# Two graph layers of 32 batches on one core: a norm's scaled mean computed on GpSimd in place of VectorE

## The chip, the core and the metric

The kernel runs on one core of a Trainium2 chip. A core has five engines, each with an instruction queue of its own that is worked off in order: TensorE (PE in the profile) for matmuls and transposes, VectorE (DVE) and ScalarE (ACT) for elementwise work and reductions, GpSimd (POOL) for small elementwise work and for issuing indirect DMAs, and SyncE (SP) for issuing plain DMAs. Engines wait for each other through semaphores. The metric is the time of one execution on the device in microseconds (us); the time of a kernel is the median of its runs.

## What is computed

The input x has 32 batches of 512 rows of 512 numbers, all float32; a matrix adj of 512 x 512 zeros and ones (on average 4 ones per row) says which rows see which. Two layers follow each other, each with a residual:

```python
h = jnp.maximum(_layernorm(x, axis=-1), 0.0)
x = x + _L0_gnn_ref(h, adj, Wq, bq, Wk, bk, Wv, bv, Wo, bo)   # 8-head attention over neighbours, out @ Wo + bo
h = jnp.maximum(_layernorm(x, axis=-1), 0.0)
x = x + _L1_gnn_ref(h, W, a, beta, adj)                       # softmax of leaky_relu(s1_i + s2_j) * adj; elu(h' + beta * h)
```

The layer norm has no weights: `(x - m) / sqrt(v + 1e-5)`, with the mean and the variance of a row. So each row needs two numbers, rstd = (v + 1e-5)^-0.5 and -m * rstd; then relu(x * rstd + (-m * rstd)) is one ScalarE instruction with a scale and a bias per row. There are 32 batches x 4 tiles x 2 layers = 256 such norms of 128 rows.

## The kernel before

Rows are sorted once by their number of neighbours, so that the neighbours of a tile of 128 rows fit into 4 gathers of 128 rows. Everything is then done for tiles of 128 rows, 4 tiles (T) a batch, 32 batches (B).

Stage A of a batch (line 767 on, `turned_state`, `queries`, `keys_and_values`): a tile of x is fetched by an indirect DMA from POOL (line 774), normed (`norm`), passed through relu on ACT (line 768) and transposed on PE (line 741, copied to SBUF by ACT at line 796). Queries are one product with Wq (line 42, bias added by DVE at line 804). Keys and values of two tiles are made together by a Strassen scheme of seven half products (line 872), with sums of the left sides on DVE (line 861) and additions of results on DVE (line 880) and copies on ACT (lines 894, 896). All three go to tables in DRAM (SP, line 911).

Stage B of a batch: for each tile, POOL gathers key and value rows (line 960, tile `kv`) and query rows (line 983, tile `qe`) edge by edge. DVE multiplies and sums (lines 1028, 1031), ACT takes the exponential (1037) and weighs the values (1042), PE sums the edges (line 1015 into bank `px`), DVE divides (1070, 1066), PE transposes (741) and multiplies with Wo (42), DVE adds the residual (1083). Then comes the second norm, relu into `hx` (768), two dot products on DVE (1091), and a store to a table (1097). Layer 1 runs two batches behind: its edge weights (lines 1157 to 1170, tile `wv`), its edge sums (1015), transposes, product with W (42), the elu (1232 on ACT, 1237 and 1238 on DVE) and an indirect store of the result from POOL (779). In the last batches the rows' s1 values go through DRAM and come back spread over partitions (lines 1130 to 1143).

The order of all this is not written by hand. The program describes each operation with `op(engine, cost, key, function, r=, w=)`: the engine, an assumed duration, a due time, and the buffers that it reads and writes. `Plan.order` then runs a list scheduler over all operations: it keeps an assumed clock for each engine, takes whichever operation can start first, prefers low keys among those that can start at the same time, and assigns the buffers of each ring as they come free. What it returns is the issue order of every engine. Inside one operation several instructions can follow each other on one engine; nothing comes between them. A change of an operation's cost, engine or number moves the assumed clocks, and so can move instructions all over the program.

The norm is three operations. The first, on DVE, is `stats`: lines 756 (statistics of 512 columns into `st`), 757 (mean and variance into columns 0 and 1 of `mv`) and 758 (variance plus epsilon into column 2). The second, on POOL, raises column 2 to the power -0.5 (line 761; `mhalf` holds -0.5). The third, on DVE again, writes column 3 = column 0 * -1 * column 2 (line 763). ACT's relu (line 768) takes column 2 as scale and column 3 as bias. The last reader of `mv` in a batch is line 1121 on DVE, which checks that mean and variance of all four tiles are finite. `mv` has 4 columns for each tile of a batch; a planned wait is for the tile's columns.

Of the kernel before, what the change touches and what calls it, by code (L numbers as in the profile page):

```python
# [12 lines left out]
ALU = mybir.AluOpType  # L13
# [51 lines left out]
class Plan:  # L65
# [14 lines left out]
    def buf(self, tag, name=""):  # L80
        return Buf(tag, name)

    def op(self, eng, us, key, fn, r=(), w=(), dma=0, form=128):
        def parts(xs):
            return [x if isinstance(x, tuple) else (x, None) for x in xs]

        r, w = parts(r), parts(w)
        o = Op(eng, us * self.PACE.get(eng, 1.0), key, fn, r, w, [], dma)
        o.form = form
        evict = eng in ("DVE", "ACT") and any(b.tag in self.free_order for b, _ in r + w)  # L90
        o.rank = key - self.FREE * evict
        for xs, write in ((r, False), (w, True)):
            for b, part in xs:
                for other, opart, owrite in b.log:
                    if (write or owrite) and other is not o and (
                        part is None or opart is None or part == opart
                    ):
                        o.before[other] = True
                b.log.append((o, part, write))
        for b in dict.fromkeys(b for b, _ in r + w):  # L100
            b.users += 1
            if b.first is None and b.tag in self.rings:
                b.first = o
                o.alloc.append(b)
            elif b.first is not None and b.first is not o:
                o.behind[b.first] = True
        self.ops.append(o)
        return o
# [110 lines left out]
def kernel(  # L219
# [23 lines left out]
    nc = tc.nc  # L243
# [7 lines left out]
    def ctile(shape, name, dt=F32):  # L251
        return const.tile(shape, dt, name=name, tag=name)

    wq, wk, wv, wo, w1 = (ctile([P, C, D], n) for n in ("wq", "wk", "wv", "wo", "w1"))
    mhalf = ctile([P, T], "mhalf")
# [50 lines left out]
    buf, op = plan.buf, plan.op  # L306
# [444 lines left out]
    def norm(key, src, mv, t, name):  # L751

        s6 = buf("st", name)

        def stats():
            nc.vector.bn_stats(s6.ap, src.ap)  # L756
            nc.vector.bn_aggr(mv.ap[:, t, 0:2], s6.ap)
            nc.vector.tensor_scalar_add(mv.ap[:, t, 2:3], mv.ap[:, t, 1:2], EPS)  # L758

        op("DVE", 1.05, key, stats, r=[src], w=[s6, (mv, t)])  # L760
        op("POOL", 0.75, key, lambda: nc.gpsimd.tensor_tensor(  # L761
            mv.ap[:, t, 2:3], mv.ap[:, t, 2:3], mhalf[:, 0:1], op=ALU.pow), w=[(mv, t)])
        op("DVE", 0.17, key, lambda: nc.vector.scalar_tensor_tensor(  # L763
            mv.ap[:, t, 3:4], mv.ap[:, t, 0:1], -1.0, mv.ap[:, t, 2:3], op0=ALU.mult, op1=ALU.mult),
           w=[(mv, t)])

    def relu(dst, src, mv, t):
        nc.scalar.activation(dst, src, AF.Relu, bias=mv[:, t, 3:4], scale=mv[:, t, 2:3])  # L768
# [13 lines left out]
    def turned_state(b, t, key, mv):  # L782
        xb = buf("x", f"x{b}_{t}")
        if b:
            op("POOL", 1.3, key - 2.0 * S, lambda: fetch(xb.ap, b, t), r=[C_["perm"]], w=[xb], dma=P * D * 4)
        else:
            op("SP", 0.1, -90.0 + 0.01 * t, lambda: nc.sync.dma_start(xb.ap, x[0, ts(t, P), :]), w=[xb], dma=P * D * 4)
        norm(key - 1.3 * S, xb, mv, t, f"a{b}_{t}")
        op("ACT", 0.8, key - 0.9 * S, lambda: relu(xb.ap, xb.ap, mv.ap, t), r=[(mv, t)], w=[xb])
        pt, hT = buf("D", "pt"), buf("hT", f"hT{b}_{t}")  # L790
        kt = key + ((0.48, -0.51)[t % 2] if b else -0.51) * S
        if b == 0 and t == 0:
            run_on(kt, 3, pt, first, 1.7)
        o = op("PE", 0.45, kt, lambda: turned(pt.ap, xb.ap), r=[xb], w=[pt])
        plan.reserve(o, hT)
        op("ACT", 0.6, kt, lambda: nc.scalar.copy(hT.ap.rearrange("p c q -> p (c q)"), pt.ap), r=[pt], w=[hT])  # L796
        return hT
# [222 lines left out]
    def layer0(b, t, kb, slots, held, qs, weights):  # L1020
# [61 lines left out]
        op("PE", 3.43, k + 0.72 * S, lambda: dense(pw.ap, oT.ap, wo), r=[oT, C_["wo"]], w=[pw])  # L1082
        op("DVE", 0.7, k + 0.9 * S, lambda: nc.vector.tensor_tensor(x1.ap, pw.ap, x1.ap, op=ALU.add), r=[pw], w=[x1])  # L1083
        norm(k + 0.9 * S, x1, s["mv1"], t, f"b{b}_{t}")
        hx = s["hx"][t] = buf("hx", f"hx{b}_{t}")
        op("ACT", 0.8, k + 1.0 * S, lambda: relu(hx.ap[:, 1 : D + 1], x1.ap, s["mv1"].ap, t),
# [404 lines left out]
```

## Time and profile before

| | |
|---|---|
| median of 3 runs | 2706.05 us (2705.66 to 2709.75) |
| profiled execution | 2724.4 us |
| its span, first to last instruction | 2722.6 us |
| granted PE clock, mean | 0.989 |
| busy PE / DVE / ACT / POOL | 98% / 75% / 71% / 67% |
| DMA | 790 MB, 290 GB/s over the span |

The profile is that of one execution. Busy time of PE counts modelled ends of pipelined matmuls, so the busy time of weight loads (PEld) is given too. "Idle before" an instruction is the time that its engine stood still before it, with what ended that idleness after the arrow. "issue" is time in which the engine waited for nothing that the profile shows. In a timeline, a row is the start in us, the duration, the engine, the line, the operation with its output and inputs, how many are merged into the row, and in brackets the idle time before it. In a table of stretches, a row is the stretch in us, its length, and then the busy time of each engine with the number of instructions, the mean granted clock of PE (1.00 is full), the share of the DMA engines' time, and GB/s. Two instructions of one engine can overlap by some tens of nanoseconds in a timeline.

### The profile page before, as it was taken

Reading aid. Unit: us, or ns where it says so; the run is one execution under the profiler, and the core shown is the slowest. Engines: PE = TensorE matmul, PEld = TensorE weight load, DVE = VectorE, ACT = ScalarE, POOL = GpSimd, SP = SyncE. Lnnn points to the kernel's source line nnn. Section 1 sums busy time; section 2 is a strip of 40 time slices with the busy share of each in tenths; the row PEclk is TensorE's granted clock in tenths of the full one; section 3 lists DMA queues with packets and bytes.
Section 4 is the critical chain, followed back from the end, with each engine's and each line's share of the span. In section 5 each row is a group of like instructions: output and inputs, shape, how many; then the busy total and the mean of one; then the engine's idle time right before and its main releaser. Section 6 shows DMA issues by size and latency. Waiting matters only on the chain.

```text
span 2722.6 us, 39798 instructions
## 1 busy us (share of the span) xinstructions
PE 2657.9 (98%) x10248; PEld 1216.0 (45%) x10248; DVE 2054.8 (75%) x5209; ACT 1931.4 (71%) x6183; POOL 1818.6 (67%) x1710
## 2 busy tenths in 40 slices
PE   9999999999999999999999999999999999999986
PEld 4444444444444444444444444444444444444432
DVE  7767777777777777777777777777777777777674
ACT  1557777687776777777777777777777777777772
POOL 2776766667766766666766766766666766666673
PEclk9999999999999999999999999999999999999998
DMA  5988888889888888888888888988888988988883
GB/s 180 259 282 315 295 301 304 285 297 311 300 296 300 298 295 315 290 293 312 300 303 303 302 296 299 312 298 295 313 296 288 323 291 299 315 292 284 304 259 107
DMA packets 237457, 790.08 MB, mean 290 GB/s; under 512 B 34667, under 2 KB 34675, under 8 KB 237222
## 3 DMA queue, kind: packets, MB, share of 16 engines
q0 software_dynamic: 156736, 644.99, 70.4%
q1 hardware_dynamic: 80486, 142.48, 14.0%
q8 instruction: 83, 1.36, 0.2%
q14 instruction: 152, 1.25, 0.1%
HBM read 617.88 MB, written 169.46 MB: 289 GB/s over the span
## 4 chain that ended last, share of the span: by engine, by line
PE 88%; issue 3%; POOL 3%; DVE 2%; DMA 2%; ACT 1%; another core or an unknown queue 0%; POOLq 0%; SPq 0%; DVEq 0%; ACTq 0%
PE pd L42 46%; PE pd L872 26%; PE pd L741 6%; PE pd L1015 4%; PE px L1015 4%; POOL kv L960 1%; PE pd L932 1%; PE pd L1111 1%; DMA qe<-qtab,qidx 1%; POOL qe L983 1%; DMA x<-in_x_dram,perm 1%; POOL x L774 0%; ACT kv L1042 0%; DMA kv<-tkv,idx 0%
## 5 line engine op out<-in xcount | busy, mean ns | idle before, releaser
L1042 ACT ACTIVATE kv<-kv 128x64 f32<-128x64 f32 x4096 | 1012.0, 336 | 5.2
L983 POOL DMA_INDIRECT qe<-qtab,qidx x512 | 546.8, 1068 | 229.9 <-issue 123.2
L960 POOL DMA_INDIRECT kv<-tab,idx x480 | 513.0, 1069 | 180.6 <-issue 119.6
L42 PE MATMUL pd<-wq,hT 128*128 128x512 f32 x1024 | 466.4, 599 | 1.3 <-ACT hT L796 1.3
L42 PE MATMUL pd<-wo,oT 128*128 128x512 f32 x1032 | 464.5, 593 | 0.0
L42 PE MATMUL pd<-w,gT 128*128 128x512 f32 x992 | 446.4, 593 | 1.4 <-DVE gT L1221 1.4
L774 POOL DMA_INDIRECT x<-in_x_dram,perm x252 | 352.0, 1397 | 85.8 <-issue 46.4
L1028 DVE TENSOR_TENSOR qe<-qe,kv 128x1024 f32<-128x1024 f32 x256 | 312.6, 1222 | 41.2 <-DMA qe<-qtab,qidx 23.4
L1031 DVE TENSOR_REDUCE s<-qe 128x16 f32<-128x1024 f32 x256 | 310.9, 1216 | 0.1
L42 PEld LDWEIGHTS pd<-wq,hT 128*128 128x128 f32 x1024 | 196.1, 193 | 246.0 <-issue 243.2
L42 PEld LDWEIGHTS pd<-wo,oT 128*128 128x128 f32 x1032 | 194.8, 190 | 240.0 <-issue 222.4
L42 PEld LDWEIGHTS pd<-w,gT 128*128 128x128 f32 x992 | 188.1, 190 | 239.7 <-issue 231.2
L761 POOL TENSOR_TENSOR mv<-mv,mhalf 128x1 f32<-128x1 f32 x256 | 171.1, 669 | 174.7 <-DVE mv L758 150.7
L779 POOL DMA_INDIRECT out_dram<-w,perm x128 | 158.5, 1238 | 153.2 <-DVE w L1238 120.1
L872 PE MATMUL pd<-wk,hT 128*128 128x512 f32 x496 | 241.5, 611 | 4.0 <-ACT hT L796 3.4
L872 PE MATMUL pd<-wt,S 128*128 128x512 f32 x496 | 237.7, 602 | 3.8 <-DVE k L880 3.7
L872 PE MATMUL pd<-wv,S 128*128 128x512 f32 x496 | 235.2, 597 | 4.1 <-DVE mv L763 2.1
L1232 ACT ACTIVATE w<-pd,dn 128x512 f32<-128x512 f32 x128 | 87.7, 685 | 178.0 <-PE pd L42 163.6
L1091 DVE CUSTOM_DVE_ANT_0 w<-hx,wa_r 128x512 f32<-128x512 f32 x256 | 175.5, 686 | 9.3 <-ACT hx L768 8.6
L756 DVE BATCH_NORM_STATS2 st<-x 128x6 f32<-128x512 f32 x256 | 176.5, 689 | 3.0 <-DMA x<-in_x_dram 0.4
L1083 DVE TENSOR_TENSOR x<-pd,x 128x512 f32<-128x512 f32 x128 | 88.1, 688 | 119.8 <-PE pd L42 86.5
L741 PEld LDWEIGHTS pd<-ident,w 128*128 128x128 f32 x1152 | 133.5, 142 | 82.7 <-issue 46.8
(213 smaller groups left out, 3569.6 us busy)
## 6 DMA issues: line engine op xcount, KB each, us to landing
qtab<-q SPq DMA_DIRECT2D x124, 258.0 KB
tab<-hx SPq DMA_DIRECT2D x120, 260.0 KB
tab<-v SPq DMA_DIRECT2D x120, 260.0 KB
tab<-k SPq DMA_DIRECT2D x120, 256.0 KB
qe<-qtab,qidx POOLq DMA_INDIRECT x512
kv<-tab,idx POOLq DMA_INDIRECT x480
x<-in_x_dram,perm POOLq DMA_INDIRECT x252
th<-hx SPq DMA_DIRECT2D x8, 260.0 KB
```

Source lines behind the costliest of these rows:

```text
L42: nc.tensor.matmul(out, lhsT, rhs, start=start, stop=stop)
L741: nc.tensor.transpose(p[:, ts(c, P)], src[:, ts(c, P)], ident)
L756: nc.vector.bn_stats(s6.ap, src.ap)
L774: nc.gpsimd.indirect_dma_start(dst, None, rows, bass.IndirectOffsetOnAxis(ap=perm[:, t : t + 1], axis=0), **lim)
L872: nc.tensor.matmul(p.ap, lhs()[:, c, :], rhs[:, c, :], start=first and c == 0, stop=c == K2 - 1, skip_group_check=True)
L960: nc.gpsimd.indirect_dma_start(dst, None, tab.ap, bass.IndirectOffsetOnAxis(ap=idx[:, t, g : g + 1], axis=0), bounds_check=N + DUMMY - 1, ...
L983: op("POOL", 1.3, kb - 0.84 * S + 0.1 * g, lambda q=qs[g // 2], g=g, t=t: nc.gpsimd.indirect_dma_start(q.ap[:, g % 2, :], None, s["qtab"]. ...
L1015: nc.tensor.matmul(out(g), lhs(g), row(slots, g, c0, n), start=True, stop=True)
L1028: nc.vector.tensor_tensor(qe.ap[:, :, 0:D], qe.ap[:, :, 0:D], sl.ap[:, :, KO : KO + D], op=ALU.mult)
L1031: nc.vector.tensor_reduce(sb.ap, qe.ap[:, :, 0:D].rearrange("p n (h f) -> p n h f", f=HD), axis=AX.X, op=ALU.add)
L1042: nc.scalar.activation(p[:, h, 0:HD], p[:, h, 0:HD], AF.Copy, scale=p[:, h, HD : HD + 1])
L1091: nc.vector.tensor_tensor_reduce(scr.ap, hx.ap[:, 1 : D + 1], row, 1.0, 0.0, op0=ALU.mult, op1=ALU.add, accum_out=dst)
```

## The change

The third operation is gone. DVE now writes column 3 = column 0 * -1 * 1 as a fourth instruction of `stats`, before the power exists, and POOL multiplies column 3 by column 2 right behind its power, in the same operation. So column 3 is complete when POOL is done, and ACT waits for POOL alone. The planner's costs change with it: `stats` from 1.05 to 1.2, POOL's operation from 0.75 to 1.3, and DVE's 0.17 is dropped. The file is two lines longer: lines behind the norm are numbered two higher after the change; the power is line 763 and the product line 764.

```diff
             nc.vector.bn_aggr(mv.ap[:, t, 0:2], s6.ap)
             nc.vector.tensor_scalar_add(mv.ap[:, t, 2:3], mv.ap[:, t, 1:2], EPS)
 
-        op("DVE", 1.05, key, stats, r=[src], w=[s6, (mv, t)])
-        op("POOL", 0.75, key, lambda: nc.gpsimd.tensor_tensor(
-            mv.ap[:, t, 2:3], mv.ap[:, t, 2:3], mhalf[:, 0:1], op=ALU.pow), w=[(mv, t)])
-        op("DVE", 0.17, key, lambda: nc.vector.scalar_tensor_tensor(
-            mv.ap[:, t, 3:4], mv.ap[:, t, 0:1], -1.0, mv.ap[:, t, 2:3], op0=ALU.mult, op1=ALU.mult),
-           w=[(mv, t)])
+            nc.vector.tensor_scalar(mv.ap[:, t, 3:4], mv.ap[:, t, 0:1], -1.0, 1.0, op0=ALU.mult, op1=ALU.mult)
+
+        def root():
+            nc.gpsimd.tensor_tensor(mv.ap[:, t, 2:3], mv.ap[:, t, 2:3], mhalf[:, 0:1], op=ALU.pow)
+            nc.gpsimd.tensor_tensor(mv.ap[:, t, 3:4], mv.ap[:, t, 3:4], mv.ap[:, t, 2:3], op=ALU.mult)
+
+        op("DVE", 1.2, key, stats, r=[src], w=[s6, (mv, t)])
+        op("POOL", 1.3, key, root, w=[(mv, t)])
```

## The prediction, made before the result was known

> **What bounds the kernel now.** I read the busy times first, then the slices, then busy time by stretch, and only then the waits, because a wait on VectorE (DVE) matters only where TensorE (PE) runs dry.
>
> ```profile
> PE 2657.9 (98%) x10248; PEld 1216.0 (45%) x10248; DVE 2054.8 (75%) x5209; ACT 1931.4 (71%) x6183; POOL 1818.6 (67%) x1710
> ...
> core 0: us, PE busy (x) PEld busy (x) DVE busy (x) ACT busy (x) POOL busy (x), PEclk, DMA share, GB/s
> ...
> 100.00:200.00 100.00, 92.82 (x316) 41.37 (x315) 68.97 (x145) 59.55 (x204) 77.77 (x71) 0.97 0.95 286
> ...
> 1500.00:1600.00 100.00, 100.00 (x388) 45.88 (x386) 78.30 (x197) 74.96 (x242) 69.48 (x66) 1.00 0.87 301
> ...
> 2600.00:2700.00 100.00, 77.03 (x320) 33.44 (x320) 60.87 (x188) 50.93 (x146) 62.59 (x58) 0.88 0.63 195
> ```
>
> PE is busy for 2657.9 of 2722.6 us, so at most 64.7 us of idle PE can be won. By stretches of 100 us: 17.8 us of it lie before 300, 8.1 between 300 and 1000, none between 1000 and 2500, 38.8 after that. In the middle weight loads take a steady 46 us of every 100, and a batch passes every 80.95 us (waits of 0.53 us at line 763 stand at 2343.49 and 2424.43, and so back). Nothing done to DVE can shorten that stretch; it can only be lengthened.
>
> Now the wait that the change removes, in the groups by line:
>
> ```profile
> L763 DVE SCALAR_TENSOR_TENSOR mv<-mv 128x1 f32<-128x1 f32 x256 | 38.1, 155 | 81.4 <-POOL mv L761 61.4 <-issue 19.7
> ...
> L761 POOL TENSOR_TENSOR mv<-mv,mhalf 128x1 f32<-128x1 f32 x256 | 171.1, 669 | 174.7 <-DVE mv L758 150.7 <-DVE mv L763 14.0 <-issue 2.7
> ```
>
> DVE stood still for 81.4 us before line 763, almost all for GpSimd's (POOL's) power. Where did PE pay? The timeline of three engines near 144 us:
>
> ```profile
> 142.95 1.03 POOL L983 DMA_INDIRECT qe<-qtab,qidx  x1 [0.30 <-issue]
> 144.00 1.09 POOL L761 TENSOR_TENSOR mv<-mv,mhalf 128x1 f32<-128x1 f32 x2
> 145.27 1.64 POOL L774 DMA_INDIRECT x<-in_x_dram,perm  x1 [0.18 <-issue]
> ...
> 144.61 0.16 DVE L763 SCALAR_TENSOR_TENSOR mv<-mv 128x1 f32<-128x1 f32 x1 [2.87 <-POOL mv L761]
> ...
> 145.35 0.69 DVE L880 TENSOR_TENSOR k<-pd,bk_r 128x512 f32<-128x512 f32 x1
> ...
> 146.09 3.06 PE L872 MATMUL pd<-wt,S 128*128 128x512 f32 x4 [3.39 <-DVE k L880]
> ```
>
> The power is stuck behind gathers on POOL, DVE waits 2.87 us for it, the addition at line 880 behind it empties a bank late, PE idles 3.39 us. I looked at every PE wait of over a microsecond for this pattern and found it four times: at 146.09 (2.87 us of DVE wait within 3.39 of PE), 164.04 (2.09 us; the two waits before it are 0.44 and 1.66), 834.85 (1.99 us, after a DVE wait of 4.04) and 2628.21 (1.52 us within 5.85):
>
> ```profile
> 2622.26 2.04 POOL L983 DMA_INDIRECT qe<-qtab,qidx  x1 [0.30 <-issue]
> 2624.32 0.58 POOL L761 TENSOR_TENSOR mv<-mv,mhalf 128x1 f32<-128x1 f32 x1
> ...
> 2624.94 0.16 DVE L763 SCALAR_TENSOR_TENSOR mv<-mv 128x1 f32<-128x1 f32 x1 [1.52 <-POOL mv L761]
> ...
> 2628.21 2.03 PE L1015 MATMUL pd<-kv,wv 128*32 128x512 f32 x8 [5.85 <-DVE wv L1170]
> ```
>
> So of 81.4 us only 2.87 + 2.09 + 1.99 + 1.52 = 8.5 us reach PE.
>
> [...] the granted clock of the 10 us slices 140:150 and 160:170, each holding one of those stalls, is 0.84 and 0.83. So a stall costs again: 1.6 + 1.7 = 3.3 us for these two. [...] the changed program does put a wait for POOL's own power before the new product.
>
> **The change part by part.**
>
> 1. DVE loses 256 scalar_tensor_tensor of 155 ns (39.7 us) and gains 256 tensor_scalar of one element, which I price by line 758, 154 ns (39.4 us): nothing. PE's 98% hides it anyway; uncovered it would be 0.3 us.
>
> 2. DVE loses the 256 waits. Ceiling on PE 8.5 us, plus 3.3 us of clock: 11.8. I count three quarters, 9 us: at both ends other things run late too. In the 90 us from 95 the DMA engines are 95% occupied, and without the stall the next to be late is the product at line 1015, whose weighing on ScalarE (ACT) ended at 180.5 when PE took it at 182.18, 1.7 us of slack.
>
> 3. POOL gains 256 products. Neither the operation nor its self-wait is in the trace. From below: a POOL memset of 128x1 takes 98 ns. From above: the power with the gap after it, 0.58 + 0.18 = 0.76 us. [...] I take 0.35 us with its wait. Queued behind it on POOL is the next gather, for which DVE's line 1028 waits, then ACT, then PE. In the middle POOL is occupied 338.5 us in 500 plus 0.30 us behind each of 44 DMAs and 0.18 behind each of 8 powers a batch (6.2 batches): 86%. Eight products a batch make 2.8 us of 80.95, so 89%; at 0.76, 93%. There it is hidden by POOL's own waits (150.7 us for statistics, 120.1 before stores). At the ends there is no cover: POOL runs back to back from 95 to 185 (10 powers) and from 2550 to 2627 (5 powers). Fifteen products of 0.35 are 5.3 us on the gathers; PE sees, I choose, 40%: +2.1 us (range 0.6 to 8).
>
> 4. The norm's chain to ACT: power, hop to DVE, 155 ns, hop becomes power, product. About even where DVE was free, shorter where it was busy. ACT's 82.2 us of waiting for line 763 becomes waiting for POOL. Line 1121, which reads all four tiles' statistics, now waits for POOL too: 32 chances for the old stall. Priced at 0, at worst 32 x 0.5 = 16 us, if it were always early.
>
> 5. The planner sorts all operations anew, since two of its costs and an operation changed. In the order as built, the PE order repeats batch by batch from 34% to 93% of its rows before, and from 33% to 80% after. So some 13% of the span, 4 to 5 batches, leave the repeating pattern. Unrepeated batches between 300 and 1000 cost 8.1 us of stalls in 700; 13% of 2722 is 354 us, so +4.1 us. Switches between whole and 32-column matmuls go from 283 to 287; one costs some 0.2 us (four matmuls of line 872 take 1.91 after one, 1.72 otherwise): +0.8.
>
> Sum against the profiled execution (2724.4 us, span 2722.6): -9 + 2.1 + 4.1 + 0.8 = -2.0. The unprofiled median is 18 us lower, 2706.05; I carry the difference over: 2704.
>
> **Rivals.** (a) *The waits were worth all they seem, and the new order is as smooth as the old*: -11.8 plus half of the 3.4 us of clock lost at 2620:2640, some -13: 2693. For it: the stalls are plain in the timeline. Against: POOL, which made the power late, stays late. (b) *POOL becomes the bound*: slower. The product[...] costs 0.76 us rather than 0.35; 15 x 0.76 = 11 us, passed on to PE at the ends, and in the middle one gather per batch comes too late for a stall of 0.3 us in some 18 batches, +5; with part 5 some +17 less a saved 5: about 2718. It decides once the product exceeds about 0.6 us. For it: 86% occupancy, queue order. Against: gathers are issued well ahead. (c) *The wait only changes engine*: ACT and line 1121 stand where DVE stood, the clock and stalls stay: 2707. For it: ACT already waits 82.2 us for the same value.
>
> **How the numbers follow.** Likeliest case 0.38 (own range 2698 to 2710), (a) 0.27, (b) 0.25, (c) 0.10. A measurement here tells 0.2%, 5.4 us, from no change. Faster: nearly all of (a) and a third of the likeliest, 0.38. Slower: most of (b) and a little of the rest, 0.26. Same: 0.36. The range takes in (a) with a little more saved, and (b) with the dearest product: 2690 to 2722.
>
> **What would show it.** Right: no idle before the new line 760 on DVE; no PE wait near 146 and 164; clock above 0.9 in those slices; weight loads still 46 per 100 us in the middle; the product on POOL near 0.25 us; POOL busy up by 60 to 90 us. Wrong: products of over 0.5 us; PE waits repeating every batch; new PE waits for line 1170 or 1066 behind late gathers; DVE idle before line 1121 (1123 in the changed file). Most likely error: part 5, since a new order may bring or lose stalls that no row of the old trace prices.

## The result: slower by 0.34%

In seven runs each the kernel before takes 2707.06 us (2705.66 to 2709.97) and the changed one 2718.79 us (2714.32 to 2720.66), medians that lie 11.7 us apart. The ratio, which isn't formed from these two medians, is 1.0034, with a 95% interval of 1.0023 to 1.0044: slower by 0.34%, some 9 us. The forecast was 2704.0 us, 2 us faster; the time lies in its range of 2690 to 2722, on the other side of no change, and at the 2718 of rival (b).

The same program differs from chip to chip (the kernel before has medians of 2707 to 2733 us below), so the ratio of every kernel below is taken against runs of the kernel before beside it on the same chip. The profile shown of before was 18 us over its unprofiled median, that of after (2717.31 us, span 2715.5) is 1.5 us under its own. Their spans aren't compared; their rows are.

From the page of the changed kernel and its busy time by stretch, the rows that answer to those shown of before (columns as there):

```profile
PE 2656.2 (98%) x10248; PEld 1215.1 (45%) x10248; DVE 2038.2 (75%) x5209; ACT 1923.5 (71%) x6183; POOL 1886.8 (69%) x1966
...
100.00:200.00 100.00, 86.26 (x285) 37.75 (x284) 63.35 (x135) 58.38 (x198) 74.32 (x80) 0.91 0.95 267
1500.00:1600.00 100.00, 100.00 (x387) 45.86 (x387) 79.26 (x201) 75.43 (x243) 73.43 (x76) 1.00 0.90 307
2600.00:2700.00 100.00, 85.14 (x344) 36.80 (x344) 63.16 (x192) 51.72 (x145) 64.67 (x65) 0.90 0.64 195
```

The middle is as full as before. In the head PE did 285 matmuls from 100 to 200 us where it had done 316, at a clock of 0.91 for 0.97. (Another execution of the kernel before did 308 there, at 0.93, so a part of that is chance.) The groups by line that the change touches:

```profile
L763 POOL TENSOR_TENSOR mv<-mv,mhalf 128x1 f32<-128x1 f32 x256 | 168.9, 660 | 119.4 <-DVE mv L760 115.5
L770 ACT ACTIVATE hx<-x,mv 128x512 f32<-128x512 f32 x128 | 105.4, 824 | 65.2 <-POOL mv L764 64.9
L764 POOL TENSOR_TENSOR mv<-mv 128x1 f32<-128x1 f32 x256 | 61.5, 240 | 20.7
L760 DVE TENSOR_SCALAR mv<-mv 128x1 f32<-128x1 f32 x256 | 36.9, 144 | 0.2 <-issue 0.2
```

VectorE waits no more: 0.2 us before its new line 760, for 81.4 us before the old line 763. The product looks cheap: 240 ns. ScalarE waits 127.9 us for it (64.9 in this row, 63.0 in that of the first norm), where it had waited 82.2 us for VectorE. What the product costs GpSimd is in no row. It is in the timeline of that engine:

```profile
163.34 0.59 POOL L763 TENSOR_TENSOR mv<-mv,mhalf 128x1 f32<-128x1 f32 x1
164.01 0.19 POOL L764 TENSOR_TENSOR mv<-mv 128x1 f32<-128x1 f32 x1
164.81 2.05 POOL L776 DMA_INDIRECT x<-in_x_dram,perm  x1 [0.61 <-issue]
```

The power ends at 163.93, the product begins 0.08 us later, is done at 164.20, and the gather behind it begins at 164.81, 0.61 us after that. Before, a gather stood 0.18 us behind a power (145.09 to 145.27 in the timeline shown there). I took all cases in which a gather came next and waited for nothing that the profile names: from the start of the power to the start of the gather it is 0.77 us in the kernel before (median of 98) and 1.51 us after (median of 64). So a norm takes 0.74 us more of GpSimd's queue. The product accounts for 0.61 of it by the medians: 0.08 of waiting for its own power, 0.19 of work, and 0.34 in the gap before the gather, which begins 0.52 us behind a product and 0.18 behind a power. The rest goes with powers that themselves took long in these cases (over 0.7 us in 29 of 64, in 8 of 98 before); with the instructions in the old order, below, it is 0.69 us in all.

### The profile page after: what moved, and what is told of

Same layout as the page of the kernel before. It is cut to its first block, busy times and chain, and to the rows that moved or that the text cites. A ratio compares the mean times of both kernels' runs of the same rounds, so it can differ in the third digit from the quotient of the medians.

```text
span 2715.5 us, 40476 instructions
## 1 busy us (share of the span) xinstructions
PE 2656.2 (98%) x10248; PEld 1215.1 (45%) x10248; DVE 2038.2 (75%) x5209; ACT 1923.5 (71%) x6183; POOL 1886.8 (69%) x1966
## 4 chain that ended last, share of the span: by engine, by line
PE 87%; DMA 3%; DVE 3%; issue 2%; POOL 2%; ACT 1%; POOLq 0%; DVEq 0%; SPq 0%; ACTq 0%
PE pd L42 46%; PE pd L874 26%; PE pd L741 6%; PE pd L1017 4%; PE px L1017 4%; DMA qe<-qtab,qidx 1%; PE pd L934 1%; PE pd L1113 1%; ACT kv L1044 1%; DMA row<-s 1%; POOL kv L962 1%; DMA x<-in_x_dram,perm 0%; POOL x L776 0%; DVE qe L1030 0%; DVE s L1033 0%
## 5 line engine op out<-in xcount | busy, mean ns | idle before, releaser
L985 POOL DMA_INDIRECT qe<-qtab,qidx x512 | 563.7, 1101 | 187.4 <-issue 113.2
L1030 DVE TENSOR_TENSOR qe<-qe,kv 128x1024 f32<-128x1024 f32 x256 | 311.8, 1220 | 53.2 <-DMA qe<-qtab,qidx 44.1
L1234 ACT ACTIVATE w<-pd,dn 128x512 f32<-128x512 f32 x128 | 87.3, 682 | 146.5 <-PE pd L42 146.4
L741 PE MATMUL pd<-ident,w 128*128 128x128 f32 x1152 | 154.9, 275 | 11.4 <-DVE w L1068 10.1
```

The source lines that it names most:

```text
L741: nc.tensor.transpose(p[:, ts(c, P)], src[:, ts(c, P)], ident)
L985: op("POOL", 1.3, kb - 0.84 * S + 0.1 * g, lambda q=qs[g // 2], g=g, t=t: nc.gpsimd.indirect_dma_start(q.ap[:, g % 2, :], None, s["qtab"]. ...
L1030: nc.vector.tensor_tensor(qe.ap[:, :, 0:D], qe.ap[:, :, 0:D], sl.ap[:, :, KO : KO + D], op=ALU.mult)
```

## The experiments

Two theories stood at first. O: the planner's new order costs the time. P: GpSimd's product does, by holding up its queue. A kernel "in the order of the kernel before" has the same instructions in the same order as that kernel on each of the five engines, but for the instructions named.

### The order, or the instructions

again is the kernel before, unchanged.

> The kernel before, unchanged, for a second profile. Its one profiled execution so far (2724.4 us) was 17 us longer than the median of its runs (2707.1), so the stalls read from it may not be those of a usual execution. Expected: 2707 us within 2, and a span near 2705 with about 17 us less idle PE than the 64.7 us of the first profile, mostly in the first 300 and the last 220 us. If the idle PE is again near 65 us, profiling itself lengthens the execution.

Measured: 0.9995 [0.9985, 1.0005] (2725.24 us against 2726.53). This is how still the measurement is. The expectation missed: this chip is slower than the first, and the idle PE is 68.5 us again. Yet this profiled execution is only 3 us over the median, and that of the changed kernel was under its own, so it doesn't follow that profiling lengthens an execution.

order_kept has the changed instructions in the old order: the planner sees the old costs and three operations, of which the third issues nothing. Against the changed kernel:

```diff
-        op("DVE", 1.2, key, stats, r=[src], w=[s6, (mv, t)])
-        op("POOL", 1.3, key, root, w=[(mv, t)])
+        op("DVE", 1.05, key, stats, r=[src], w=[s6, (mv, t)])
+        op("POOL", 0.75, key, root, w=[(mv, t)])
+        op("DVE", 0.17, key, lambda: None, w=[(mv, t)])
```

> The changed instructions (DVE's -mean with the statistics, POOL's product behind its power) in exactly the order of the kernel before: the planner still sees the three old operations with the old costs, but the third one issues nothing. Theory O (the planner's new order costs the time, the instructions themselves are neutral or a gain): 2700 to 2708 us, so 11 us or more under the changed kernel. Theory P (POOL's product delays the gathers, whatever the order): 2714 to 2722 us, as slow as the changed kernel.

Measured: 1.0038 [1.0023, 1.0052]. The old order with the new instructions is as slow as the change, so the new order is not needed to explain it.

before_cost and after_cost change a planned cost alone (`0.75` to `0.80` in the kernel before, `1.3` to `1.0` in the changed one).

> The instructions of the kernel before, with one assumed cost moved: the power 0.80 instead of 0.75. Nothing but the planner's order changes. Theory O: any small change of the order moves the time by several us, so at least 4 us away from 2707 on either side. Theory P: 2707 within 3 us.

> The instructions of the changed kernel, with POOL's operation planned at 1.0 instead of 1.3, nearer to the measured 0.58 + 0.19 us and their gaps. Only the order changes. Theory O: away from 2719 by 4 us or more, more likely below it, since the new order was an unlucky one. Theory P: 2719 within 3 us.

Measured: 1.0083 [1.0069, 1.0098] and 1.0066 [1.0049, 1.0083]. Orders do matter, as theory O had it and theory P had not: 0.05 us in one planned cost cost the kernel before 0.83% with not an instruction changed. For after_cost theory O had expected a gain, and it is a loss.

after_again is the changed kernel beside other runs.

> The changed kernel itself, beside the others on one chip: +0.2 to +0.45% by all theories, as in its first measurement (+0.34%). The question is whether its order makes it better or worse than the same instructions in the order of the kernel before, which were +0.38% in their call: within 0.15% of that, the planner's new order is worth about nothing either way.

Measured: 1.0036 [1.0025, 1.0047], against 1.0038 in the old order. In total the two orders are worth the same.

### The removed wait, without the product on GpSimd

act_product, in the old order: VectorE takes -mean with the statistics as in the change, GpSimd makes the power alone, ScalarE the product.

```diff
     def relu(dst, src, mv, t, first=True):
+        if first:
+            nc.scalar.activation(mv[:, t, 3:4], mv[:, t, 3:4], AF.Copy, scale=mv[:, t, 2:3])
         nc.scalar.activation(dst, src, AF.Relu, bias=mv[:, t, 3:4], scale=mv[:, t, 2:3])
```

> The order of the kernel before, with nothing added on GpSimd: -mean is taken by VectorE with the statistics as in the change, and the product with the power is made by ScalarE (one activation of 128x1) right ahead of its relu, so that nothing comes back to VectorE and GpSimd's queue is as before. Theory W: the removed waits are a gain again, -0.4 to 0%. Theory C: the chain loses its hop over VectorE and gains a short activation, -0.3 to +0.1%. Theory T: +0.2 to +0.5%. The 256 activations are 50 us of ScalarE (at about 0.2 us, an estimate), which has 29% idle.

Measured: 0.9974 [0.9962, 0.9985], faster than both kernels. The 256 small activations take 0.30 us each, 76.3 us of ScalarE, where 0.2 was expected (the author's estimate; in the kernel before the 128x4 activation of line 1163 takes 0.196). Theory T, that any change of durations costs in the old order, is out: it said +0.2% or more. act_again is the same kernel on another chip.

> The product on ScalarE in the order of the kernel before once more: -0.4 to -0.1% (-0.26% before), if its gain is no accident of one call.

Measured: 0.9984 [0.9976, 0.9991]. So taking the product off both other engines is worth 0.16 to 0.26%, 4 to 7 us.

act_planned is the same with the planner told of it.

```diff
-        op("DVE", 1.05, key, stats, r=[src], w=[s6, (mv, t)])
+        op("DVE", 1.2, key, stats, r=[src], w=[s6, (mv, t)])
         op("POOL", 0.75, key, root, w=[(mv, t)])
-        op("DVE", 0.17, key, lambda: None, w=[(mv, t)])
...
-        op("ACT", 0.8, key - 0.9 * S, lambda: relu(xb.ap, xb.ap, mv.ap, t), r=[(mv, t)], w=[xb])
+        op("ACT", 1.0, key - 0.9 * S, lambda: relu(xb.ap, xb.ap, mv.ap, t), r=[(mv, t)], w=[xb])
```

The relu of the second norm goes from 0.8 to 1.0 likewise.

> The product on ScalarE as in the kernel that was 0.26% faster than before, but with the order left to the planner: statistics planned at 1.2 us, the power at 0.75 us, no third operation, the relu at 1.0 us. If the old order is a good one by luck, as the kernels with other planned costs say (+0.7 to +0.8% for 0.05 us of a power), this one gives back its gain: +0.1 to +0.7%. If the planner does as well with the true costs: -0.4 to -0.1%.

Measured: 1.0099 [1.0080, 1.0118], worse than the range expected. The gain of a version holds for an order, and the planner's next order may lose it four times over.

### What in the product costs

pool_extra is the kernel before, with a product behind the power that nobody reads.

```diff
+        def root():
+            nc.gpsimd.tensor_tensor(mv.ap[:, t, 2:3], mv.ap[:, t, 2:3], mhalf[:, 0:1], op=ALU.pow)
+            nc.gpsimd.tensor_tensor(junk, mhalf[:, 1:2], mv.ap[:, t, 2:3], op=ALU.mult)
...
-        op("POOL", 0.75, key, lambda: nc.gpsimd.tensor_tensor(
-            mv.ap[:, t, 2:3], mv.ap[:, t, 2:3], mhalf[:, 0:1], op=ALU.pow), w=[(mv, t)])
+        op("POOL", 0.75, key, root, w=[(mv, t)])
```

> The kernel before, its order on every engine, with one GpSimd product more behind each of the 256 powers; it goes to a scratch column that nobody reads, and VectorE keeps its scalar_tensor_tensor and its wait. Theory W (GpSimd's work: the products hold the queue, and the gathers behind them come late): as slow as the changed instructions in the same order were, +0.3 to +0.6%. Theory C (the chain: the factors reach ScalarE later than by VectorE): nothing of that chain is touched but the power's neighbour, so -0.1 to +0.15%. Theory T (the old order fits the old durations, and any change of durations at that order costs): +0.2 to +0.5%.

Measured: 1.0073 [1.0058, 1.0087]. No chain is longer, VectorE's wait is there as before, and the kernel is slower by twice the change's loss. Theory C, that the factors reach ScalarE late, can't explain it. It is dearer than order_kept by 0.35% (by 0.24% where both were measured again, below), which agrees with the removed wait's worth.

two_products is order_kept with this product behind its own.

```diff
             nc.gpsimd.tensor_tensor(mv.ap[:, t, 3:4], mv.ap[:, t, 3:4], mv.ap[:, t, 2:3], op=ALU.mult)
+            nc.gpsimd.tensor_tensor(junk, mhalf[:, 1:2], mv.ap[:, t, 2:3], op=ALU.mult)
```

> The changed instructions in the order of the kernel before, with a second GpSimd product into a scratch column behind the first. Theory W: twice the cost of one, +0.6 to +1.0% over the kernel before. Theory C: the second product stands behind the one that ScalarE waits for, so as with one, +0.3 to +0.5%. Theory T: no order by dose, anywhere from +0.2 to +0.8%.

Measured: 1.0048 [1.0033, 1.0063]. A miss for theory W as it was put: the second product cost 0.10% where the first had cost 0.64% (from -0.26 to +0.38). From power to gather it is 1.49 us (median) for 1.46 with one product, so the second moves the gather by 0.03. (In the mean it is 1.79 for 1.65.) So it isn't the count of instructions. Theory C had this number right, and is out by pool_extra.

indep_extra takes the power out of pool_extra's product, which then needn't wait for it.

```diff
-            nc.gpsimd.tensor_tensor(junk, mhalf[:, 1:2], mv.ap[:, t, 2:3], op=ALU.mult)
+            nc.gpsimd.tensor_tensor(junk, mhalf[:, 1:2], mhalf[:, 2:3], op=ALU.mult)
```

> As the kernel with one GpSimd product more behind each power (+0.73%), but the product reads two columns of a constant and not the power, so that GpSimd needn't wait for its own power. There the next gather began 1.44 us (median) after its power where nothing was between, 0.77 us in the kernel before. Theory D (the wait on its own result: the queue stands still until the power has ended[...]): the power to gather time falls back to 0.77 to 1.0 us, and the whole to +0.0 to +0.25%. Theory W (one instruction more on GpSimd, of whatever kind): 1.3 us or more again, and +0.5 to +0.8%.

Measured: 1.0023 [1.0013, 1.0033], and 0.98 us from power to gather. With the wait two thirds of pool_extra's cost are gone (half, by the 0.48% at which pool_extra was measured again, below).

late_product is order_kept with the product put behind the next thing in GpSimd's queue.

A norm's product is owed from its power on; it is issued behind the next operation on GpSimd, or right ahead of its relu if that comes first.

```diff
-            nc.gpsimd.tensor_tensor(mv.ap[:, t, 3:4], mv.ap[:, t, 3:4], mv.ap[:, t, 2:3], op=ALU.mult)
+            owed.append((mv.ap, t))
...
     def relu(dst, src, mv, t):
+        pay([(mv, t)])
...
         for o in todo:
+            due = list(owed) if o.eng == "POOL" else []
             o.fn()
+            pay(due)
```

order_kept_2 is order_kept again, beside it on the same chip.

> The changed instructions in the order of the kernel before, but GpSimd's product is put behind the next thing in GpSimd's queue (a gather or a store in 160 cases, another power in most of the rest) and no longer right behind its power. The wait on its own power is then over by the time the product is reached[...]; in exchange ScalarE gets its bias about 1.3 us later. Theory D (the wait on its own result is what costs): of the price of the product (0.64%, from +0.38% here to -0.26% on ScalarE) about a third stays, -0.15 to +0.15%. Theory W (the 256 instructions themselves): as right behind the power, +0.3 to +0.5%. Theory C (ScalarE's relu waiting on GpSimd costs): more than that, +0.5% and up.

> The changed instructions in the order of the kernel before once more, beside the one with the late product: +0.25 to +0.5% by all theories (+0.38% before).

Measured: 1.0026 [1.0015, 1.0037] for late_product, 1.0024 [1.0014, 1.0035] for order_kept_2 beside it. A miss for theory D: from power to gather it was 0.82 us, and the time hadn't moved. In the trace of late_product ScalarE waits longer instead:

```profile
L780 ACT ACTIVATE hx<-x,mv 128x512 f32<-128x512 f32 x128 | 104.9, 820 | 122.1 <-POOL mv L757 122.1
```

With 72.5 us in the other norm it waits 194.6 us for the product, 87.6 in order_kept_2. Whether GpSimd's wait had been the cost, with its gain given back here, or had never mattered, took three more runs.

no_self_wait is order_kept with a constant for the power in the product; the norm's right shift is left out. late_extra is pool_extra with its product put behind the next thing in the queue, as in late_product, and read by nobody. pool_extra_2 is pool_extra again.

```diff
-            nc.gpsimd.tensor_tensor(mv.ap[:, t, 3:4], mv.ap[:, t, 3:4], mv.ap[:, t, 2:3], op=ALU.mult)
+            nc.gpsimd.tensor_tensor(mv.ap[:, t, 3:4], mv.ap[:, t, 3:4], mhalf[:, 1:2], op=ALU.mult)
```

> The changed instructions in the order of the kernel before, but GpSimd's product multiplies -mean by a constant and no longer by the power (the norm's shift is then -mean times -0.5: this part of the result is left out). GpSimd doesn't wait for its own power; instructions, queues and ScalarE's wait for the product stay. Theory D (the wait on its own result, and the gap it leaves before the next gather): power to gather 1.0 us (median, from 1.46), and 0.3 to 0.5% off the +0.24 to +0.38% of the changed instructions: -0.25 to +0.05%. Theory W (the instruction of whatever kind, or ScalarE's wait): +0.2 to +0.4% as before.

> The kernel before with one GpSimd product more that reads the power and is read by nobody, put behind the next thing in GpSimd's queue. VectorE and ScalarE wait for nothing new, so that this is the late product without its late bias. Theory D: at most what the product cost that doesn't read the power, 0 to +0.25%; then the late product of the run before lost on ScalarE (194.6 us of waiting for GpSimd, 89.8 right behind the power) what it won on GpSimd. Theory W: +0.5 to +0.8%, as right behind the power.

> The product right behind its power that reads the power and is read by nobody, once more, on one chip with the late one: +0.5 to +0.85% by all theories (+0.73% before).

Measured: 0.9987 [0.9979, 0.9996], 1.0016 [1.0009, 1.0023] and 1.0048 [1.0032, 1.0063]. Theory D holds in both pairs. With the same instructions on the same engines in the same order, and ScalarE waiting for the same product, taking away GpSimd's wait on its own power turned 0.24 to 0.38% slower (order_kept, on two other chips) into 0.13% faster. And a product that nobody reads cost 0.16% where its wait was over when it was reached, 0.48% where it wasn't, both on one chip. Two norms side by side in the timeline, first of order_kept (GpSimd, and what ScalarE and TensorE make of it):

```profile
148.22 0.59 POOL L763 TENSOR_TENSOR mv<-mv,mhalf 128x1 f32<-128x1 f32 x1
148.90 0.19 POOL L764 TENSOR_TENSOR mv<-mv 128x1 f32<-128x1 f32 x1
149.05 0.55 POOL L763 TENSOR_TENSOR mv<-mv,mhalf 128x1 f32<-128x1 f32 x1
149.12 0.81 ACT L771 ACTIVATE hx<-x,mv 128x512 f32<-128x512 f32 x1 [4.81 <-POOL mv L764]
149.67 0.19 POOL L764 TENSOR_TENSOR mv<-mv 128x1 f32<-128x1 f32 x1
149.84 0.56 ACT L799 COPY hT<-pd 128x512 f32<-128x512 f32 x1
150.42 1.74 POOL L777 DMA_INDIRECT x<-in_x_dram,perm  x1 [0.55 <-issue]
150.46 1.60 PE L875 MATMUL pd<-wk,hT 128*128 128x512 f32 x2 [1.92 <-ACT hT L799]
```

then the same two of no_self_wait (GpSimd alone):

```profile
143.69 0.58 POOL L763 TENSOR_TENSOR mv<-mv,mhalf 128x1 f32<-128x1 f32 x1
144.24 0.18 POOL L764 TENSOR_TENSOR mv<-mv,mhalf 128x1 f32<-128x1 f32 x1
144.39 0.55 POOL L763 TENSOR_TENSOR mv<-mv,mhalf 128x1 f32<-128x1 f32 x1
144.91 0.18 POOL L764 TENSOR_TENSOR mv<-mv,mhalf 128x1 f32<-128x1 f32 x1
145.26 1.63 POOL L777 DMA_INDIRECT x<-in_x_dram,perm  x1 [0.17 <-issue]
```

From the first power to the gather: 2.20 us in one, 1.57 in the other, and 1.27 in the prediction's timeline of the kernel before, all with the same queue. The plain product begins 0.03 us before its power ends, and the gather stands 0.17 us behind it; the waiting one begins 0.07 to 0.09 us after the power's end, and the gather stands 0.55 us behind it. Whether the wait could be dropped isn't shown: no run here leaves it out and keeps the right result.

The first of the two traces also shows the stall of 146 us that the change was to remove. ScalarE stands 4.81 us there for GpSimd, and TensorE waits 1.92 us for ScalarE's copy. ScalarE had stood at this place before, for VectorE's line 763; the row of the kernel before:

```profile
144.80 0.82 ACT L768 ACTIVATE hx<-x,mv 128x512 f32<-128x512 f32 x1 [3.37 <-DVE mv L763]
```

So the power comes late behind its gathers in both; VectorE is out of the chain, and of TensorE's 3.39 us at this place 1.92 stay.

Not every product takes 0.19 us. In order_kept 49 of the 256 take over 0.6 us, up to 1.25. Of these, 33 began while VectorE's product of line 1031 was running (1028 before), 16 while its line 1240 was (1237 before), both with two inputs from SBUF, and each of the 49 ended 0.05 us behind that instruction. None of the other 207 began inside line 1031's product. Under one with an input from PSUM this wasn't seen: products that began inside line 1069's `w<-px,rd`, with 0.46 to 0.67 us of it left, kept their 0.19 us. One of the 49:

```profile
583.31 1.23 DVE L1031 TENSOR_TENSOR qe<-qe,kv 128x1024 f32<-128x1024 f32 x1 [1.00 <-DMA x<-in_x_dram,perm]
583.34 1.25 POOL L764 TENSOR_TENSOR mv<-mv 128x1 f32<-128x1 f32 x1
```

The changed kernel has 18 such products, 8 that began inside its line 1030 and 10 inside its line 1239, all ended 0.05 us behind it. Do the long products, rather than the wait, make the difference? The first pair can't tell: the 256 products take 86.7 and 80.0 us in order_kept and order_kept_2, 61.5 us in no_self_wait. The second pair can: late_extra, which costs a third of pool_extra_2, has more long products (31 over 0.6 us for 8, and 74.0 us for 57.2 in all). So the long products are there, and the cost doesn't follow them.

Which wait do the late gathers lengthen? One is that of VectorE's product of line 1028. In pool_extra_2 and in late_extra, the same group by line:

```profile
L1032 DVE TENSOR_TENSOR qe<-qe,kv 128x1024 f32<-128x1024 f32 x256 | 312.4, 1222 | 82.9 <-DMA qe<-qtab,qidx 60.7 <-DMA kv<-tab,idx 19.0 <-issue 2.1
```

```profile
L1041 DVE TENSOR_TENSOR qe<-qe,kv 128x1024 f32<-128x1024 f32 x256 | 312.6, 1222 | 45.4 <-DMA qe<-qtab,qidx 36.5 <-issue 4.6 <-DMA kv<-tab,idx 2.9
```

82.9 us idle before it with the wait on the power, 45.4 without. So it goes in most: 77.1 (order_kept), 87.3 (order_kept_2), 72.9 (two_products) and 87.8 us (pool_extra) with it, 48.5 (again), 41.6 (no_self_wait), 45.0 (late_product) and 37.0 (act_again) without. But indep_extra, without it, has 71.3. And most of the difference lies where it costs little. From 1000 to 2500 us, in the same two kernels:

```profile
L1032 DVE TENSOR_TENSOR qe<-qe,kv 128x1024 f32<-128x1024 f32 x149 | 182.2, 1223 | 51.8 <-DMA qe<-qtab,qidx 37.7 <-DMA kv<-tab,idx 13.3
```

```profile
L1041 DVE TENSOR_TENSOR qe<-qe,kv 128x1024 f32<-128x1024 f32 x149 | 182.1, 1222 | 19.6 <-DMA qe<-qtab,qidx 17.5 <-DMA kv<-tab,idx 1.3
```

Of 37.5 us more, 32.2 fall into this stretch, in which TensorE doesn't run dry in either kernel. Outside it 31.1 us stand against 25.8, and the faster no_self_wait has 32.8. So this wait shows that the gathers come late; it isn't shown to be the way by which TensorE loses its time.

### Where it is lost

ends_only and middle_only have the changed norm in the first 25 and last 11 norms alone, and in the 220 between alone; the others are as before, the order too.

```diff
+            made.append(name)
+            if not 25 < len(made) <= 245:
+                on_pool.append(1)
+                nc.vector.tensor_scalar(mv.ap[:, t, 3:4], mv.ap[:, t, 0:1], -1.0, 1.0, op0=ALU.mult, op1=ALU.mult)
...
+            if on_pool:
+                nc.gpsimd.tensor_tensor(mv.ap[:, t, 3:4], mv.ap[:, t, 3:4], mv.ap[:, t, 2:3], op=ALU.mult)
...
+            if not on_pool:
+                nc.vector.scalar_tensor_tensor(
+                    mv.ap[:, t, 3:4], mv.ap[:, t, 0:1], -1.0, mv.ap[:, t, 2:3], op0=ALU.mult, op1=ALU.mult)
```

In middle_only the condition is the opposite one.

> The order of the kernel before; the changed norm (product on GpSimd, nothing back to VectorE) in the first 25 and the last 11 norms alone, that is up to about 260 us and from about 2490 us on; the 220 between are as before. Theory E (the product costs where GpSimd is saturated, as the prediction's part 3 has it, and is covered in the middle): nearly the whole cost, +0.25 to +0.5%. Theory S (it costs all along, some per batch): -0.1 to +0.15%.

> The other way round: the first 25 and the last 11 norms as before, the 220 between changed, in the order of the kernel before. Theory E: -0.1 to +0.1%, as TensorE is busy all through the middle. Theory S: +0.2 to +0.45%.

Measured: 1.0032 [1.0021, 1.0043] and 1.0017 [1.0008, 1.0026]. Neither theory has it whole: 36 norms at the ends cost 8.7 us, 0.24 us each; 220 cost 4.6 us, 0.02 us each. The middle covers most of the product, but not all. The busy times by stretch of order_kept_2 show where PE falls behind:

```profile
0.00:300.00 300.00, 278.39 (x954) 127.53 (x955) 217.68 (x539) 155.74 (x500) 184.47 (x207) 0.95 0.80 255
300.00:1000.00 700.00, 691.51 (x2683) 317.27 (x2682) 531.60 (x1360) 520.72 (x1680) 505.92 (x517) 1.00 0.88 300
```

and of act_again, on the same chip:

```profile
0.00:300.00 300.00, 281.15 (x971) 129.13 (x972) 220.83 (x544) 168.55 (x543) 183.71 (x181) 0.97 0.80 260
300.00:1000.00 700.00, 695.68 (x2690) 318.92 (x2689) 536.96 (x1373) 543.28 (x1771) 487.24 (x452) 1.00 0.88 304
```

17 matmuls less in the head, where the granted clock is 0.95 for 0.97, and 4.2 us of PE less from 300 to 1000 us. From 1000 to 2500 both have PE busy for 1500.00 us with 5860 matmuls. The same matmuls start 4.6 us later by 242 us (241.91 for 237.33), 10.4 by 2557 (2556.56 for 2546.19) and 15.1 by 2682 (2682.02 for 2666.90); this pair of single executions is 16.2 us apart, their medians 10.1.

## Why the prediction was wrong

- **What bounds the kernel: right.** From 1000 to 2500 us PE is busy for 1499.76 us after the change; weight loads took 45.86 us of 100, as said.
- **Part 1, the exchange on VectorE: right.** The new instruction takes 144 ns for the 154 priced.
- **Part 2, the removed waits, -9 of at most 11.8 us: the size about holds.** (3.3 us of the 11.8 are the author's estimate from the clock of two slices, 0.84 and 0.83.) With the product on ScalarE they are worth 4 to 7 us net of its 256 activations; where GpSimd has the product in both (pool_extra against order_kept, and the two again) 0.24 to 0.35%, 6.5 to 9.5 us. The mechanism was half right: near 146 us, in the old order, VectorE no longer waits, but ScalarE still stands for the late power, as rival (c) had it, and part of TensorE's stall stays.
- **Part 3, the product on GpSimd, +2.1 us: this is the step that failed.** "I take 0.35 us with its wait" was 0.69 to 0.74 of GpSimd's queue. In TensorE's time, +2.1 us was 13 to 20 us: pool_extra and pool_extra_2, which add such a product and take away nothing, are slower by 0.73 and 0.48%. (From act_product to order_kept it is 0.64%, 17 us, and from act_again to order_kept_2 0.40%, 11 us.) It asked what the product takes and put it, as the author's estimate, between a memset's 98 ns and 0.76 us; the work is 0.19 us where none of VectorE's products holds it up. What it left out is what stands behind: a gather begins 0.18 us behind a power and 0.52 behind a product that has waited for the power. Why it begins later there isn't shown. The upper bound, 0.76 us, was taken from a row that had this gap in it, the power with the 0.18 behind it, and was close. The price was off by a factor of two; the rest is the share that reaches TensorE, put at 40% of fifteen products. But 36 at the ends cost 8.7 us even with their removed waits in the sum, and the middle, which was "hidden", 4.6. (Nor does GpSimd run quite back to back from 2550 to 2627 us: it waits three times for VectorE there, 3.2 us.)
- **Part 4, the chain, 0 us: right for line 1121's 32 chances** (line 1123 now waits 0.0 us), and for ScalarE in the old order, where its wait is 80.4 us (order_kept) for 85.3 (again). In the new order it grew from 82.2 to 127.9 us, though the ratio to the kernel before is about the same. That such a wait isn't free late_product suggests: with 107 us more of it than order_kept_2 it was no faster, though its gathers came earlier.
- **Part 5, the new order, +4.9 us: not seen in the total** (1.0034 and 1.0036 in the new order, 1.0038 and 1.0024 in the old). "Most likely error: part 5" named the wrong part. But other planned costs moved the time by 0.30% (after_cost against the change), 0.83% (before_cost) and 1.25% (act_planned against act_product), 8 to 34 us where 4.9 were priced; this time the new order happened to cost nothing.
- **The rivals.** (b) is nearest to what happened: slower, by a product that costs about 0.76 us of the queue, and gathers that come late. That its 2718 is the measured time to 1 us is luck: its terms (11, 5, part 5's 4.9, less 5) make 16 us and not 12, and one of them, the new order's, didn't come in the total. In the middle the gathers do come late (line 1028's product waits 43.3 us from 1000 to 2500 us in order_kept_2, 25.2 in again), but TensorE stands still for 0.0 us there in order_kept_2, 2.0 in middle_only. Products that VectorE holds up exist, 18 over 0.6 us in the changed kernel and 49 in order_kept, but the cost doesn't follow them; it lies in the wait and the gap.
- **The signs.** Nearly all that was to show the forecast right came true: no idle before line 760, clock 1.00 in the slices of 140 and 160 us, a product "near 0.25 us" (0.24), POOL up by 68 us. They watched the row of the product, and the cost lay between rows. The PE waits came elsewhere than said: 6.95 us at 130.87 and 4.36 at 192.25, where the clocks of the 10 us slices are 0.65 and 0.66.

What stays open: GpSimd's wait was taken away in the old order alone. That it is the cost in the planner's new order too is argued from the equal ratio, not shown; there the gathers are less late (53.2 us before line 1030) and ScalarE waits longer. By which wait a late gather reaches TensorE isn't shown: in ends_only, which loses 8.7 us, line 1028's product waits no longer than before (41.9 us), and in middle_only, which loses 4.6, it waits 83.5 us. That a late product costs by way of ScalarE is argued from late_product, not tested alone. A planner's order for the product on ScalarE that keeps its gain wasn't found.

## What to carry to other kernels

Price an instruction on a queue by the time from its predecessor's start to its successor's, not by its own row: one that must wait for the result just ahead of it on the same engine can also lengthen the gap before the next one, here by 0.34 us. A value wanted by a third engine may be best finished there: with a small activation on ScalarE this kernel was 0.16 to 0.26% faster than before, in the old order alone. And before a change is compared under a planner, put it into the old order once: otherwise a lottery of some 1% is read as its effect.

## What the runs showed of the hardware

- On GpSimd, a product of 128x1 that reads the power just ahead (changed kernel): 0.08 us of wait, 0.19 of work, the next gather 0.52 us behind it. One that doesn't read it (no_self_wait): no wait, 0.18, and the gather 0.16 us behind (medians of 64 and 101 cases).
- A second small product behind the waiting one (two_products) cost little: it moved the gather by 0.03 us in the median, 0.14 in the mean, and the kernel by 0.10%, within the intervals of both.
- A product of 128x1 on GpSimd that began during VectorE's 128x1024 product of two SBUF inputs ended 0.05 us behind it, in all 33 cases of order_kept, and took up to 1.25 us for 0.19. In those that began during line 1069's product with an input from PSUM, with 0.46 to 0.67 us of it left, it kept its 0.19 us.
- In the kernel before, a gather that waits for nothing the profile names begins 0.30 us behind another gather (median of 823), 0.18 behind a power (median of 98).
- The unchanged kernel has medians of 2707, 2727, 2724, 2733, 2710 and 2711 us in six sets of runs on at least four chips, the third and fourth of them on one chip: up to 1% between chips, 0.3% on one.
- An activation of 128x1 on ScalarE takes 0.30 us (act_product, act_again).
